# Bias copied into accumulators, and the weight loads of a two-MLP block reordered

## The chip, the cores and the metric

The kernel runs on one core of a Trainium2 chip. The metric is the device time of one execution in microseconds (us), the median of several runs. TensorE is written PE, VectorE DVE, ScalarE ACT, GpSimd POOL and SyncE SP.

## The reference

The input x has 32 sequences of 128 tokens with 512 features, so 4096 rows; cond gives one row of 512 per sequence, and mask marks some tokens of each sequence. All is float32.

```python
emb = silu(t) @ ada_w + ada_b
shift, scale, gate_msa = split(emb, 3)
norm = layernorm(x) * (1 + scale[:, None]) + shift[:, None]
norm = where(m, norm, 0)
fwd = gelu(norm @ ssm_w1 + ssm_b1) @ ssm_w2 + ssm_b2           # exact gelu
bwd = gelu(norm @ bwd_w1 + bwd_b1) @ bwd_w2 + bwd_b2           # the flips cancel
x = x + gate_msa[:, None] * where(m, fwd + bwd, 0)
ff_ada = silu(t) @ ffada_w + ffada_b
shift_mlp, scale_mlp, gate_mlp = split(ff_ada, 3)
ff_norm = layernorm(x) * (1 + scale_mlp[:, None]) + shift_mlp[:, None]
h = gelu_tanh(ff_norm @ ff_w1 + ff_b1)
out = x + gate_mlp[:, None] * (h @ ff_w2 + ff_b2)
```

ssm_w1, bwd_w1, ssm_w2 and bwd_w2 are 512 x 512; ff_w1 is 512 x 1024 and ff_w2 is 1024 x 512. The first two MLPs act on masked tokens only, the last one ("the second MLP" of the change) on all tokens.

## The kernel before

**Two parts.** The opening (to about 94 us) computes fwd + bwd for the masked tokens alone. They are numbered in slots; 512 slots in four tiles of 128 are handled in the straight program, and a loop at the end of the program would take further ones. The main part then runs the second MLP over four pairs of two groups of four sequences. Its two matrix products use a scheme of seven block products in place of eight (P1 to P7), applied twice in the first product, so sums and differences of blocks of weights and of tokens are made beforehand on VectorE.

**Order.** The schedule is written by hand: within each engine, instructions run in program order. Functions such as `hidden` and `project` take dictionaries that say behind which step another operation is placed. All loads of weights go through SP's queue in program order. [...]

**The opening, step by step.**

- Slots are counted, the first two tiles of rows are gathered from x (`xc`), and modulation rows `mod1` are computed on PE. `of_slots` multiplies a 0/1 matrix by modulation rows and so gives each slot its sequence's shift, scale or gate, in PSUM; `modulated_by_strips` applies them on VectorE. `xn_late` are the tiles 2 and 3 after that.
- `hidden` and `hidden_of_tile` (L207, L644) give the hidden layers, 8 blocks of 128 features: 4 of fwd, 4 of bwd. `w2` holds ssm_w2 in its first four blocks and bwd_w2 in its last four. `gates_of_slots` makes the gates `gs` of all four tiles.
- `project` (L224) sums the 8 blocks of a tile into one PSUM bank, 16 records for one tile. The pool ps_o has three banks, ps_h three, ps_t two.
- The bias of the projection is b2 + b2b, which is added to b2 on VectorE (L761). `with_gated_bias` (L348, L349) multiplies it by the gate and adds it to the tile's rows of x, for each of the four tiles. `finish_slots` (tiles 0 and 1: L354, L355 and statistics) and `finish_late` (tiles 2 and 3: L1342, L1343) multiply the projection by the gate, add the rows and store them.
- Tiles 0 and 1 are stored with their mean and root into `x1_wide`. POOL waits for both stores and then gathers them over the eight sequences of pair 0 in `take_first_half` (L813), of whose rows only the masked ones are replaced.
- `fw1` and `fw2` are ff_w1 and ff_w2. `Weights.combine` (L376) makes block differences of them, `weight_sums` (L703) makes further ones, and `store_weight_sums` writes these to DRAM (`t_rows`), from where the main part reads them as `tw`.
- ffada_w gives `mod2` (L301 with pm_f), which `transposed_modulation` transposes (`ptr_mod`, L793) into modT.
- The eight sequences of pair 0 are normalised (L838). Side 0 (four sequences) is transposed in 32 x 32 blocks on VectorE and its rows are reordered by 16 DMAs (`turned`, half on SP, half on ACT), then scaled on ACT (L878). Side 1 is transposed on PE (`turn(k)`, L884), each of the four transposing 128 features of all four sequences, and scaled on VectorE (L876). `TokenBlocks.one` (L925) makes block sums, and the first product starts (L1056).

**Where the loads stand before.** SP's queue holds, after the conditioning weights and the first layers: two pairs of sequences (`load_raw`), ssm_w2, bwd_w2, the two biases, fw1 in one load, two more pairs, ffada_w, its biases, then stores of tiles 0 and 1 and of weight sums 3. fw2 is loaded in eight parts, each behind one gather: a POOL memset of one element (L139) makes it wait for the gather's issue.

**What is placed where.** Side 1's turns and the row DMAs before stand so:

```python
after = {4 + b: [turn_rows(b)] for b in range(4)}
after[0] = [transposed_modulation]
after[1] = [lambda: weight_sums(2)]
...
po_s2 = project(0, h1, w2, "s2", {2: turn(0), 4: turn(1), 6: turn(2)})
finish_late(2, po_s2)
po = project(1, h1, w2, "s3", {0: turn(3)}, (ps_h, "h"))
```

Of the kernel before, what the change touches and what calls it, by code (L numbers as in the profile page):

```python
# [22 lines left out]
def kernel(  # L23
# [193 lines left out]
    def project(i, h, w, name, between=None, bank=(ps_o, "o")):  # L217

        pool, tag = bank
        po = pool.tile([P, 512], F32, tag=tag, name=f"po_{name}_{i}")  # L220
        for f in range(HC):
            if between and f in between:
                between[f]()
            nc.tensor.matmul(po, h[f][:, ts(i, P)], w[:, f, :], start=(f == 0), stop=(f == HC - 1))  # L224
        return po
# [77 lines left out]
    def of_slots(picked, tiles, mod, kinds, banks, name):  # L303

        n = kinds.stop - kinds.start
        t = [
            pool.tile([P, 512], F32, tag=tag, name=f"{name}_{j}")[:, : len(tiles) * n * P].rearrange(
                "p (a m c) -> p a m c", m=n, c=P
            )
            for j, (pool, tag) in enumerate(banks)  # L310
        ]
        for at, c in enumerate(tiles):
            for j in range(KC):
                nc.tensor.matmul(
                    t[j][:, at],
                    picked[ts(j, B), ts(c, P)],
                    mod[ts(j, B), kinds],
                    start=True,
                    stop=True,
                )  # L320
        return t
# [14 lines left out]
    def gates_of_slots(tiles):  # L336
# [5 lines left out]
        for j in range(KC):  # L342
            nc.scalar.copy(t[:, :, ts(j, P)], strips[j][:, :, 0])
        return [t[:, n] for n in range(len(tiles))]

    def with_gated_bias(at, gate):
        t = tp.tile([P, D], F32, tag="t", name=f"bg_s_{at}")
        nc.vector.tensor_tensor(t, b2, gate, ALU.mult)  # L348
        nc.vector.tensor_tensor(xc[at], xc[at], t, ALU.add)  # L349

    def finish_slots(at, h1, gate):
        t = tp.tile([P, 1, D + 2], F32, tag="t", name=f"t_s_{at}")
        row = t[:, 0, :D]
        nc.vector.tensor_tensor(row, project(at, h1, w2, f"s{at}"), gate, ALU.mult)  # L354
# [215 lines left out]
    load_raw(1)  # L570
    load_blocks(w2[:, :KC], ssm_w2)
    load_blocks(w2[:, KC:], bwd_w2)
# [50 lines left out]
    b2 = ssm.tile([P, D], F32, name="b2")  # L623
    b2b = tp.tile([P, D], F32, tag="t", name="b2b")
    fb2 = const.tile([P, D], F32, name="fb2")
    for t, vec in ((b2, ssm_b2), (b2b, bwd_b2)):
        broadcast_rows(t, vec, nc.sync)
    nc.sync.dma_start(fw1, ff_w1.rearrange("(k p) f -> p k f", p=P))
# [5 lines left out]
    load_conditioning_bias(modb_f, ffada_b, range(3), nc.sync)  # L634
    ph_s = {}
# [45 lines left out]
    def in_blocks(t):  # L681
        return t.rearrange("p g (h f) -> p (g h) f", f=2 * P)
# [52 lines left out]

# [7 lines left out]
    for n in range(2):  # L743
# [5 lines left out]
    xn_late = [  # L749
        modulated_by_strips(  # L750
            xc[2 + c], strips, c, spare[1][:, c], mv_t[:, c, 0:1], rstd_t[:, c : c + 1]
        )
        for c in range(2)
    ]
    h1 += hidden(xT_s, NH, w1, 0, AF.Gelu, "s0", ssm, range(KC, HC))
    gs = gates_of_slots(range(NC))
    fw1_of = Weights(fw1, KC // 2, FF // 2, t_1)
    fw1_of.combine(0, 1, 2, 3)
    for n in range(2, 4):
        own_statistics(raw[n], 2, f"x_{n}")  # L760
    nc.vector.tensor_tensor(b2, b2, b2b, ALU.add)  # L761
    b2_row = dram.tile([1, D], F32, name="b2_row")
    for c in range(2):
        with_gated_bias(c, gs[c])
    finish_slots(0, h1, gs[0])
    total, start_at, more_i, col_l = count_more()
    for c in range(2, NC):
        with_gated_bias(c, gs[c])
    finish_slots(1, h1, gs[1])
# [8 lines left out]
    modulation_matmuls(pm, ada_f, 0, 3, range(KC))  # L778
    modulation_rows(pm, mod2, modb_f, 0, 3)
    t = in_blocks(group_of_tiles("tw_3"))  # L780
    t_sum[3] = [t[:, :4], t[:, 4:]]
    weight_sums(3)
    store_weight_sums(3)
# [3 lines left out]
    weight_sums(1)  # L787
# [21 lines left out]
    def take_first_half(p, xs, which=range(2 * G), behind=None):  # L809
        slots = NH if p == 0 else NS  # L810
        for i in which:
# [9 lines left out]
            if behind:  # L821
                behind(i)
# [464 lines left out]
    def load_fw2_part(k):  # L1287
        load_behind_gathers(fw2[:, k : k + 1], ff_w2[ts(k, P)])

    take_first_half(0, x_of[0], range(2 * G), load_fw2_part)  # L1290
# [28 lines left out]
    def combine_behind_weight_sums():  # L1319
# [4 lines left out]
    after = {4 + b: [turn_rows(b)] for b in range(4)}  # L1324
    after[0] = [transposed_modulation]
    after[1] = [lambda: weight_sums(2)]
    after[4].insert(0, normalised_of_side_0)
    after[7] += [
        normalised_of_side_1,
        lambda: weight_sums(4),  # L1330
        combine_behind_weight_sums,
        lambda: store_weight_sums(4, 1, 2),
        lambda: x_of.update({1: [load_side(1, 0, spare), None]}),
    ]
# [5 lines left out]
    def finish_late(at, po):  # L1340
        t = tp.tile([P, D], F32, tag="t", name=f"t_s_{at}")
        nc.vector.tensor_tensor(t, po, gs[at], ALU.mult)  # L1342
        nc.vector.tensor_tensor(t, t, xc[at], ALU.add)  # L1343
        nc.sync.dma_start(x1_rows[ts(at, P), :], t)

    po_s2 = project(0, h1, w2, "s2", {2: turn(0), 4: turn(1), 6: turn(2)})
    finish_late(2, po_s2)
    po = project(1, h1, w2, "s3", {0: turn(3)}, (ps_h, "h"))
# [3 lines left out]
    finish_late(3, po)  # L1352
# [288 lines left out]
```

## Time and profile before

| what | value |
|---|---|
| median of 3 runs | 464.37 us (464.25 to 467.19) |
| the profiled execution's own time | 466.65 us |
| its span, first to last instruction | 464.9 us |
| mean granted TensorE clock | 0.992 |
| PE busy | 448.4 us (96%) |
| DVE busy | 334.7 us (72%) |
| ACT busy | 175.4 us (38%) |
| POOL busy | 163.5 us (35%) |
| moved by DMA | 70.96 MB, mean 153 GB/s |

The profile is of one execution, and its clock starts at the span's start. "Idle before, releaser" in its lines is the time that an engine stood still before an instruction and what ended it. The granted clock is 1.00 at full speed. A DMA's time to landing runs from its issue to its last completion.

### The profile page before, as it was taken

What the parts mean: (1) busy time and instruction counts of PE and PEld (TensorE: products, weight loads), DVE (VectorE), ACT (ScalarE), POOL (GpSimd) and SP (SyncE); (2) the same over time, 40 slices, a digit from 0 to 9 for tenths busy, and PEclk for the clock granted to TensorE, in tenths of its full rate; (3) what the DMA queues carried; (4) which work ended last, traced back from release to release, by engine and by line L of the source; (5) the groups of instructions that cost most, each with busy time, mean ns of one, the idle gap of its engine ahead of it and who ended that gap; (6) DMA issues with size and microseconds to landing.
All of it is one profiled execution on the core that took longest, in us unless ns stands there. A gap on an engine that the chain in (4) does not pass through costs nothing.

```text
span 464.9 us, 6219 instructions
## 1 busy us (share of the span) xinstructions
PE 448.4 (96%) x2160; PEld 371.7 (80%) x2160; DVE 334.7 (72%) x573; ACT 175.4 (38%) x384; POOL 163.5 (35%) x161
## 2 busy tenths in 40 slices
PE   8999878989999999999999999999999999999996
PEld 3785465468888888888888888888888888888884
DVE  4676986779869857996687489967873996433645
ACT  3121110465365273254543723535537144562000
POOL 4210146418964000289720004897100025660000
PEclk9999979999999999999999999999999999999999
DMA  7999269974405661934067529330764342222022
GB/s 232 383 394 401 80 177 210 273 273 150 158 9 187 99 123 43 338 115 163 3 206 103 100 70 340 100 145 2 222 98 89 125 169 80 79 77 106 0 82 103
DMA packets 83468, 70.96 MB, mean 153 GB/s; under 512 B 63224, under 2 KB 64584, under 8 KB 82410
## 3 DMA queue, kind: packets, MB, share of 16 engines
q1 hardware_dynamic: 68502, 58.61, 40.7%
q0 software_dynamic: 4160, 10.54, 6.6%
q10 hardware_dynamic: 10772, 1.39, 2.1%
q8 instruction: 18, 0.29, 0.2%
q14 instruction: 16, 0.13, 0.1%
HBM read 56.84 MB, written 13.70 MB: 152 GB/s over the span
## 4 chain that ended last, share of the span: by engine, by line
PE 78%; DMA 7%; DVE 7%; issue 2%; ACT 2%; SPq 1%; POOL 1%; POOLq 0%; DVEq 0%
PE a_o L1243 23%; PE a_m L1056 19%; PE e_o L1243 18%; PE e_m L1056 15%; DMA fw<-in_L_cond_ff_w_dram 3%; DMA ada_a<-in_L_cond_ada_w_dram 2%; ACT xT L878 1%; POOL x L813 1%; DMA x<-x_wide,slot_i 1%; DMA t_rows<-x 1%; PE ph_s L644 1%; DVE t L376 1%; PE last L1243 1%; DMA x_wide<-t_s 1%; DVE xc L349 1%
## 5 line engine op out<-in xcount | busy, mean ns | idle before, releaser
L1107 POOL TENSOR_TENSOR ha<-p_m,ha 128x512 f32<-128x512 f32 x20 | 25.8, 1288 | 166.6 <-ACT ha L1114 157.3
L1243 PE MATMUL e_o<-fw,ha 128*128 128x256 f32 x256 | 57.9, 379 | 0.0
L878 ACT ACTIVATE xT<-xT,modT 128x128 f32<-128x128 f32 x112 | 44.1, 480 | 34.8 <-DMA xT<-xn 31.4
L1243 PE MATMUL a_o<-t,hb 128*128 128x256 f32 x240 | 54.1, 379 | 0.0
L1243 PEld LDWEIGHTS e_o<-fw,ha 128*128 128x128 f32 x256 | 48.6, 190 | 6.6
L1243 PEld LDWEIGHTS a_o<-t,hb 128*128 128x128 f32 x240 | 45.6, 190 | 6.2
L1018 ACT ACTIVATE hb<-hb,biasT 128x256 f32<-128x256 f32 x64 | 29.0, 501 | 27.9 <-POOL hb L1140 19.3
L1070 ACT COPY p_m<-e_m 128x512 f32<-128x512 f32 x27 | 15.8, 585 | 46.8 <-PE e_m L1056 46.8
L813 POOL DMA_INDIRECT x<-x_rows,slot_i x24 | 27.6, 1148 | 6.3 <-issue 5.1
L1107 POOL TENSOR_TENSOR hb<-p_m,hb 128x512 f32<-128x512 f32 x20 | 29.4, 1469 | 0.3
L1243 PE MATMUL a_o<-fw,ha 128*128 128x256 f32 x128 | 28.9, 379 | 0.0
L1243 PE MATMUL a_o<-t,s 128*128 128x256 f32 x128 | 28.9, 379 | 0.0
L1243 PE MATMUL e_o<-fw,s 128*128 128x256 f32 x128 | 28.9, 379 | 0.0
L224 PE MATMUL po_s<-w,h_s 128*128 128x512 f32 x64 | 28.6, 594 | 0.0
L1114 ACT COPY ha<-e_m 128x512 f32<-128x512 f32 x32 | 18.5, 579 | 25.7 <-PE e_m L1056 25.2
L1243 PEld LDWEIGHTS e_o<-fw,s 128*128 128x128 f32 x128 | 24.3, 190 | 3.3
L1243 PEld LDWEIGHTS a_o<-t,s 128*128 128x128 f32 x128 | 24.3, 190 | 3.3
L1243 PEld LDWEIGHTS a_o<-fw,ha 128*128 128x128 f32 x128 | 24.3, 190 | 3.3
L1081 DVE TENSOR_TENSOR e_m<-a_m,ha 128x512 f32<-128x512 f32 x20 | 13.9, 696 | 16.7 <-POOL ha L1107 6.6
L1018 ACT ACTIVATE ha<-e_m,biasT 128x256 f32<-128x256 f32 x48 | 20.0, 468 | 15.6 <-PE e_m L1056 14.3
L1056 PE MATMUL e_m<-s,fw 128*128 128x256 f32 x92 | 23.8, 382 | 1.7 <-DVE e_m L1081 1.7
L1056 PE MATMUL a_m<-xT,tw 128*128 128x256 f32 x96 | 24.6, 379 | 0.0
(235 smaller groups left out, 902.2 us busy)
## 6 DMA issues: line engine op xcount, KB each, us to landing
tw<-t_rows SPq DMA_DIRECT2D x16, 896.0 KB, 5.3
x<-in_x_dram SPq DMA_DIRECT2D x16, 512.0 KB, 6.6
gate<-gate_rows POOLq DMA_DIRECT2D x8, 1024.0 KB, 5.1
out_dram<-x SPq DMA_DIRECT2D x15, 512.0 KB, 3.2
xT<-xn SPq DMA_DIRECT2D x92, 64.0 KB, 2.3
ada_f<-in_L_cond_ffada_w_dram SPq DMA_DIRECT2D x4, 768.0 KB, 14.8
ada_a<-in_L_cond_ada_w_dram SPq DMA_DIRECT2D x4, 512.0 KB, 5.5
w<-in_L_cond_ssm_w_dram SPq DMA_DIRECT2D x2, 1024.0 KB, 7.8
```

The source lines that it names most:

```text
L224: nc.tensor.matmul(po, h[f][:, ts(i, P)], w[:, f, :], start=(f == 0), stop=(f == HC - 1))
L349: nc.vector.tensor_tensor(xc[at], xc[at], t, ALU.add)
L376: engine.tensor_tensor(out, x, y, ALU.subtract)
L813: nc.gpsimd.indirect_dma_start(out=raw[i // 2][:, i % 2] if p == 0 else xs[i // G][i % G // 2][:, i % 2], out_offset=None, in_=x1_rows if ...
L878: nc.scalar.activation(out, src, AF.Identity, bias=shift, scale=scale)
L1018: nc.scalar.activation(dst[:, n], src[:, n], AF.Gelu_apprx_tanh, bias=biasT[:, f : f + 1])
L1056: nc.tensor.matmul(bank[:, ts(n, QT)], self.w_block(j, product)[:, ts(n, P)], self.x_block(j, product), start=(product in ("P1", "P5") and ...
L1070: nc.scalar.copy(p5, e)
L1081: nc.vector.tensor_tensor(e, a, p5, add)
L1107: nc.gpsimd.tensor_tensor(self.place(RESULT[j], c), self.p5[j], other, ALU.add)
L1114: nc.scalar.copy(self.place(RESULT[j], c), src)
L1243: nc.tensor.matmul(part, src[:, k, ts(i, P)], w[product][:, k, :], start=(last and k == 0), stop=True, skip_group_check=True,)
```

## The change

Seven edits, all in the opening.

1. The bias goes into the accumulators. `seeded_with_bias` copies b2 (already with b2b added) by ACT into a bank of ps_o, for tiles 0, 1 and 2, and `project` then accumulates onto it without a start flag. Tile 3, in a bank of ps_h, gets the bias by one VectorE addition in `finish_late`. `with_gated_bias` is gone. The first seed is copied between the gates' matmuls and the copies of the gates, the two others behind them.
2. `of_slots` starts only on the first tile of a bank.
3. b2 and b2b are loaded before ssm_w2, and added between the two tiles of xn_late.
4. fw1 is loaded before bwd_w2. Its combination, weight sums 3 and their store stand before `finish_slots(0)`, and the statistics of the later pairs behind it.
5. fw2 is loaded in two halves: one behind ffada_w and its biases, one behind the stores of tiles 0 and 1. The loads behind gathers and their memsets are gone.
6. Weight sums 1 stand before mod2's rows and are stored there; weight sums 2 are stored where they are made. `count_more` moves up.
7. The row DMAs of side 0 stand later (behind hidden blocks 5, 6, 7), side 1's turns each two blocks earlier (in front of blocks 0, 2, 4 and 6 of project 2).

```diff
@@ -214,14 +214,26 @@
                 g()
         return h
 
-    def project(i, h, w, name, between=None, bank=(ps_o, "o")):
+    def project(i, h, w, name, between=None, bank=(ps_o, "o"), seeded=None):
 
         pool, tag = bank
-        po = pool.tile([P, 512], F32, tag=tag, name=f"po_{name}_{i}")
+        po = seeded or pool.tile([P, 512], F32, tag=tag, name=f"po_{name}_{i}")
         for f in range(HC):
             if between and f in between:
                 between[f]()
-            nc.tensor.matmul(po, h[f][:, ts(i, P)], w[:, f, :], start=(f == 0), stop=(f == HC - 1))
+            nc.tensor.matmul(
+                po,
+                h[f][:, ts(i, P)],
+                w[:, f, :],
+                start=(f == 0 and seeded is None),
+                stop=(f == HC - 1),
+                skip_group_check=seeded is not None,
+            )
+        return po
+
+    def seeded_with_bias(at):
+        po = ps_o.tile([P, 512], F32, tag="o", name=f"po_s{at}")
+        nc.scalar.copy(po, b2)
         return po
 
     def gated(po, bias, gate, name):
@@ -315,8 +327,9 @@
                     t[j][:, at],
                     picked[ts(j, B), ts(c, P)],
                     mod[ts(j, B), kinds],
-                    start=True,
+                    start=(at == 0),
                     stop=True,
+                    skip_group_check=True,
                 )
         return t
 
@@ -339,19 +352,17 @@
             pick, tiles, mod1, slice(2, 3), 2 * [(ps_o, "o")] + 2 * [(ps_t, "tr")], f"gate_s{tiles[0]}"
         )
         t = ssm.tile([P, len(tiles), D], F32, tag="gs", name=f"gs_{tiles[0]}")
-        for j in range(KC):
-            nc.scalar.copy(t[:, :, ts(j, P)], strips[j][:, :, 0])
-        return [t[:, n] for n in range(len(tiles))]
-
-    def with_gated_bias(at, gate):
-        t = tp.tile([P, D], F32, tag="t", name=f"bg_s_{at}")
-        nc.vector.tensor_tensor(t, b2, gate, ALU.mult)
-        nc.vector.tensor_tensor(xc[at], xc[at], t, ALU.add)
-
-    def finish_slots(at, h1, gate):
+
+        def to_sbuf():
+            for j in range(KC):
+                nc.scalar.copy(t[:, :, ts(j, P)], strips[j][:, :, 0])
+
+        return [t[:, n] for n in range(len(tiles))], to_sbuf
+
+    def finish_slots(at, po, gate):
         t = tp.tile([P, 1, D + 2], F32, tag="t", name=f"t_s_{at}")
         row = t[:, 0, :D]
-        nc.vector.tensor_tensor(row, project(at, h1, w2, f"s{at}"), gate, ALU.mult)
+        nc.vector.tensor_tensor(row, po, gate, ALU.mult)
         nc.vector.tensor_tensor(row, row, xc[at], ALU.add)
         own_statistics(t, 1, f"s_{at}_x1")
         nc.sync.dma_start(x1_wide[ts(at, P), :], t[:, 0])
@@ -568,8 +579,11 @@
 
     load_raw(0)
     load_raw(1)
+    b2 = ssm.tile([P, D], F32, name="b2")
+    b2b = tp.tile([P, D], F32, tag="t", name="b2b")
+    for t, vec in ((b2, ssm_b2), (b2b, bwd_b2)):
+        broadcast_rows(t, vec, nc.sync)
     load_blocks(w2[:, :KC], ssm_w2)
-    load_blocks(w2[:, KC:], bwd_w2)
     pick_slots(1)
 
     slot_of = adap.tile([B, S], F32, name="slot_of")
@@ -620,18 +634,16 @@
     fw2 = fwp.tile([P, HC, D], F32, name="fw2")
     t_1 = fwp.tile([P, 3, KC // 2, FF // 2], F32, name="t_1")
     t_2 = fwp.tile([P, 3, HC // 2, D // 2], F32, name="t_2")
-    b2 = ssm.tile([P, D], F32, name="b2")
-    b2b = tp.tile([P, D], F32, tag="t", name="b2b")
     fb2 = const.tile([P, D], F32, name="fb2")
-    for t, vec in ((b2, ssm_b2), (b2b, bwd_b2)):
-        broadcast_rows(t, vec, nc.sync)
-    nc.sync.dma_start(fw1, ff_w1.rearrange("(k p) f -> p k f", p=P))
+    load_blocks(fw1, ff_w1)
+    load_blocks(w2[:, KC:], bwd_w2)
     load_raw(2)
     load_raw(3)
     ada_f = adap.tile([P, KC, 3 * D], F32, tag="ada", name="ada_f")
     modb_f = adap.tile([P, 3, P], F32, tag="modb", name="modb_f", bufs=1)
     load_ada(ada_f, ffada_w, range(KC), 3 * D)
     load_conditioning_bias(modb_f, ffada_b, range(3), nc.sync)
+    load_blocks(fw2[:, :KC], ff_w2[:D])
     ph_s = {}
 
     def hidden_of_tile(f, c):
@@ -732,7 +744,7 @@
         nc.vector.tensor_scalar(col_l, slot_col[:, 0:1], start_at, None, ALU.add)
         return total, start_at, more_i, col_l
 
-
+    total, start_at, more_i, col_l = count_more()
     h1 = []
     for f in range(KC):
         hidden_of_tile(f, 1)
@@ -746,27 +758,32 @@
     strips = of_slots(
         pick, (2, 3), mod1, slice(0, 2), 3 * [(ps_o, "o")] + [(ps_t, "tr")], "part_s2"
     )
-    xn_late = [
-        modulated_by_strips(
-            xc[2 + c], strips, c, spare[1][:, c], mv_t[:, c, 0:1], rstd_t[:, c : c + 1]
+    xn_late = []
+    for c in range(2):
+        xn_late.append(
+            modulated_by_strips(
+                xc[2 + c], strips, c, spare[1][:, c], mv_t[:, c, 0:1], rstd_t[:, c : c + 1]
+            )
         )
-        for c in range(2)
-    ]
+        if c == 0:
+            nc.vector.tensor_tensor(b2, b2, b2b, ALU.add)
     h1 += hidden(xT_s, NH, w1, 0, AF.Gelu, "s0", ssm, range(KC, HC))
-    gs = gates_of_slots(range(NC))
+    gs, gates_to_sbuf = gates_of_slots(range(NC))
+    po_s = [seeded_with_bias(0)]
+    gates_to_sbuf()
+    po_s += [seeded_with_bias(at) for at in (1, 2)]
     fw1_of = Weights(fw1, KC // 2, FF // 2, t_1)
     fw1_of.combine(0, 1, 2, 3)
+    t = in_blocks(group_of_tiles("tw_3"))
+    t_sum[3] = [t[:, :4], t[:, 4:]]
+    weight_sums(3)
+    store_weight_sums(3)
+    b2_row = dram.tile([1, D], F32, name="b2_row")
+    finish_slots(0, project(0, h1, w2, "s0", seeded=po_s[0]), gs[0])
     for n in range(2, 4):
         own_statistics(raw[n], 2, f"x_{n}")
-    nc.vector.tensor_tensor(b2, b2, b2b, ALU.add)
-    b2_row = dram.tile([1, D], F32, name="b2_row")
-    for c in range(2):
-        with_gated_bias(c, gs[c])
-    finish_slots(0, h1, gs[0])
-    total, start_at, more_i, col_l = count_more()
-    for c in range(2, NC):
-        with_gated_bias(c, gs[c])
-    finish_slots(1, h1, gs[1])
+    finish_slots(1, project(1, h1, w2, "s1", seeded=po_s[1]), gs[1])
+    load_blocks(fw2[:, KC:], ff_w2[D:])
     nc.sync.dma_start(b2_row, b2[0:1, :])
     broadcast_rows(fb2, ff_b2, nc.sync)
 
@@ -776,15 +793,12 @@
     mod2 = const.tile([P, 3, P], F32, name="mod2")
     pm = ps_h.tile([P, 512], F32, tag="h", name="pm_f")
     modulation_matmuls(pm, ada_f, 0, 3, range(KC))
+    weight_sums(1)
+    store_weight_sums(1)
     modulation_rows(pm, mod2, modb_f, 0, 3)
-    t = in_blocks(group_of_tiles("tw_3"))
-    t_sum[3] = [t[:, :4], t[:, 4:]]
-    weight_sums(3)
-    store_weight_sums(3)
     early.close()
     xtp = straight.enter_context(tc.tile_pool(name="xtp", bufs=1, side="right"))
     sp = straight.enter_context(tc.tile_pool(name="sp", bufs=1, side="right"))
-    weight_sums(1)
     modT = const.tile([P, KC, 2 * B], F32, name="modT")
 
     def transposed_modulation():
@@ -806,7 +820,7 @@
     fw2_of = Weights(fw2, HC // 2, D // 2, t_2)
 
 
-    def take_first_half(p, xs, which=range(2 * G), behind=None):
+    def take_first_half(p, xs, which=range(2 * G)):
         slots = NH if p == 0 else NS
         for i in which:
             b = 2 * p * G + i
@@ -818,8 +832,6 @@
                 bounds_check=slots - 1,
                 oob_is_err=False,
             )
-            if behind:
-                behind(i)
 
     def gate_tile(p, side):
         t = gp.tile([P, G, D], F32, tag=f"g{side}", name=f"gate_{p}_{side}", bufs=1)
@@ -1284,10 +1296,7 @@
                 self.store(c, 1)
 
 
-    def load_fw2_part(k):
-        load_behind_gathers(fw2[:, k : k + 1], ff_w2[ts(k, P)])
-
-    take_first_half(0, x_of[0], range(2 * G), load_fw2_part)
+    take_first_half(0, x_of[0])
     xT = [new_xT(0, side) for side in range(2)]
     gate_rows = dram.tile([B, D], F32, name="gate_rows")
     for j in range(KC):
@@ -1321,35 +1330,40 @@
         nc.gpsimd.tensor_copy(done, t_sum[4][1][0:1, 2, 0:1])
         fw2_of.combine(0, 1, engine=nc.gpsimd)
 
-    after = {4 + b: [turn_rows(b)] for b in range(4)}
-    after[0] = [transposed_modulation]
-    after[1] = [lambda: weight_sums(2)]
-    after[4].insert(0, normalised_of_side_0)
-    after[7] += [
-        normalised_of_side_1,
-        lambda: weight_sums(4),
-        combine_behind_weight_sums,
-        lambda: store_weight_sums(4, 1, 2),
-        lambda: x_of.update({1: [load_side(1, 0, spare), None]}),
-    ]
+    after = {
+        0: [transposed_modulation, lambda: weight_sums(2), lambda: store_weight_sums(2)],
+        3: [normalised_of_side_0],
+        5: [turn_rows(0)],
+        6: [normalised_of_side_1, turn_rows(1)],
+        7: [
+            turn_rows(2),
+            turn_rows(3),
+            lambda: weight_sums(4),
+            combine_behind_weight_sums,
+            lambda: store_weight_sums(4),
+            lambda: x_of.update({1: [load_side(1, 0, spare), None]}),
+        ],
+    }
     h1 = hidden(xT_t, NH, w1, 0, AF.Gelu, "s1", ssm, after=after)
     nc.scalar.activation(warm, biasT[0:1, 0:1], AF.Gelu_apprx_tanh)
     for k in range(KC):
         scaled(0, xT[0], k)
 
-    def finish_late(at, po):
+    def finish_late(at, po, bias=None):
         t = tp.tile([P, D], F32, tag="t", name=f"t_s_{at}")
+        if bias is not None:
+            nc.vector.tensor_tensor(t, po, bias, ALU.add)
+            po = t
         nc.vector.tensor_tensor(t, po, gs[at], ALU.mult)
         nc.vector.tensor_tensor(t, t, xc[at], ALU.add)
         nc.sync.dma_start(x1_rows[ts(at, P), :], t)
 
-    po_s2 = project(0, h1, w2, "s2", {2: turn(0), 4: turn(1), 6: turn(2)})
-    finish_late(2, po_s2)
-    po = project(1, h1, w2, "s3", {0: turn(3)}, (ps_h, "h"))
+    finish_late(2, project(0, h1, w2, "s2", {2 * k: turn(k) for k in range(KC)}, seeded=po_s[2]))
+    po = project(1, h1, w2, "s3", bank=(ps_h, "h"))
     of_x[0] = TokenBlocks(0, xT)
     for j in (1, 2, 3, 4):
         of_x[0].one(j)
-    finish_late(3, po)
+    finish_late(3, po, b2)
     first_half.close()
     hp = straight.enter_context(tc.tile_pool(name="hp", bufs=1))
     gp = straight.enter_context(tc.tile_pool(name="gp", bufs=1))
```

## The prediction

> **What bounds the kernel now.** First the table of stages (busy time of each engine per stretch) and the page's busy row: from 110 us on TensorE has no gap worth naming until the tail, so a change in the opening is worth what it moves the start of that stretch, one for one, and no more than TensorE loses before it.
>
> ```profile
> PE 448.4 (96%) x2160; PEld 371.7 (80%) x2160; DVE 334.7 (72%) x573; ACT 175.4 (38%) x384; POOL 163.5 (35%) x161
> ...
> 50.00:60.00 10.00, 6.11 (x50) 3.31 (x48) 9.45 (x24) 1.67 (x5) 0.55 (x1) 0.93 0.15 56
> 60.00:70.00 10.00, 9.04 (x33) 7.69 (x34) 8.48 (x15) 1.42 (x3) 5.28 (x8) 0.73 0.72 213
> ...
> 110.00:120.00 10.00, 10.00 (x48) 8.75 (x48) 9.77 (x20) 5.21 (x10) 8.76 (x8) 1.00 0.16 32
> ```
>
> Columns: stretch, length, then busy time (count) of PE, PEld, DVE, ACT, POOL, then PE clock, DMA share, GB/s. From 50 to 70 VectorE is full, TensorE is not, its clock falls. The DMA view of 30 to 62 us (40 slices of 0.8 us) shows a pause of transfers there, with the full rate of about 410 until 46 us and a thin rest until 52.4:
>
> ```profile
> GB/s 410 415 410 410 410 410 410 392 392 392 412 399 422 433 384 438 407 415 422 407 207 131 106 93 52 20 19 5 0 0 0 98 382 177 0 0 0 0 0 139
> ```
>
> Next TensorE's waits up to 112 us (in total, times, longest):
>
> ```profile
> PE ptr_mod L793 <- DVE mod L301: 4.8, 1, 4.8
> PE ptr L884 <- DVE xn L838: 2.3, 2, 1.3
> PE e_m L1056 <- DVE e_m L1081: 1.7, 2, 1.1
> PE e_m L1056 <- ACT e_m L1102: 0.5, 1, 0.5
> ```
>
> Who makes VectorE late is in the chain (start, length, what) and in the timeline:
>
> ```profile
> 24.92 14.40 DMA fw<-in_L_cond_ff_w_dram
> ...
> 60.88 2.98 DMA x_wide<-t_s
> ...
> 75.14 4.42 DMA x<-x_wide,slot_i
> ...
> 60.35 0.56 DVE L301 TENSOR_TENSOR mod<-pm_f,modb_f 128x384 f32<-128x384 f32 x1
> 60.96 0.69 PE L793 MATMUL ptr_mod<-ident,mod 128*128 128x128 f32 x2 [4.85 <-DVE mod L301]
> 61.44 14.19 PE L207 MATMUL ph_s<-xT_s,w 128*128 128x256 f32 x56
> ...
> 80.19 0.33 PE L884 MATMUL ptr<-ident,xn 128*128 128x128 f32 x1 [1.34 <-DVE xn L838]
> 93.69 1.03 PE L1056 MATMUL a_m_alone<-xT,fw 128*128 128x256 f32 x4
> ```
>
> So the order is: fw1 lands at 39.3; VectorE combines it, adds gated biases and finishes two tiles until 60.1; only then is mod ready (TensorE idle 4.85) and the second tile stored; the store lands at 63.87, eight gathers follow to 79.56, and project 2 goes on behind turn(0) at 80.35. The first product begins at 93.69 and loses 2.9 us more up to its group at 107.79: that group starts 14.1 after 93.69, where 13 groups of 0.863 are 11.2.
>
> **What the Trainium skill says.** "TensorE: Matmul & The Clock Gate", Part 1: the clock halves after an idle activity window of about 3.4 us, and windows run freely. The trace agrees: with one idle stretch of 4.85 us the clock was 0.50 over 58.54:65.37, in which TensorE worked 4.41 us, so 2.2 us were lost. "DMA: Bandwidth & Descriptors", "Queues, rings and completion order": each DMA engine takes one queue's descriptors in ring order and alternates between queues by packets. No row shows that per engine; it fits the fw1 load, which was issued at 24.92 and landed 14.4 later with the queue full. "PSUM — Partial Sum Buffer", "The four PSUM rules": a matmul without the first-flag accumulates onto what another engine wrote where the bank's bits are set, which is why of_slots now keeps its start flag for the first tile; this costs no instruction. The copy's price comes from the trace:
>
> ```profile
> L1182 ACT COPY a_o<-fb x8: 575/585/592, 133.5 to 416.5; 128x512 f32<-128x512 f32 x8
> L224 PE MATMUL po_s<-w,h_s 128*128 128x512 f32 x64 | 28.6, 594 | 0.0
> ```
>
> **The change part by part.** Times below are on the profile's clock.
>
> 1. Loads. fw1 goes ahead of bwd_w2 (1024 KB). The DMA view shows 410 GB/s here, so it lands 2.6 earlier, about 36.8. bwd_w2 lands where fw1 did, 39.3; project 0 wants it at its fifth block, at 40.8 (below), so 1.5 us cover it. b2 and b2b only pass ssm_w2, which has over 6 us to spare. SP runs well ahead of the data (fw1 issued at 24.92), so the moved issues cost nothing.
>
> 2. Bias. Eight L348/L349 operations leave VectorE (about 0.65 each in sequence: 5.3 us). One addition (0.69) comes on the late tile path and b2 + b2b goes between the two tiles of xn_late (0.62). Three ScalarE copies of 0.58 come in; ScalarE waits 12.50 us before its L199 copy at 51.07, which hides them. The moved addition is not free: the gates of L314 reuse the banks that the second tile reads, so the gates end at 37.3 for 36.67, and both projections (16 records of 0.433 each, 6.9 us) end at 44.2 and 51.1, not 50.44. Seed 0 waits for the same tile (35.8), is done at 36.4 and is not late.
>
> 3. VectorE, 36.8 on. Combine 5.0 to 41.8, weight sums 3 (1.28 + 0.95, less overlap: 2.1) to 43.9. finish_slots(0) now waits for TensorE at 44.2 and takes 2.5, to 46.8; statistics of two raw pairs 3.6, to 50.4; finish_slots(1) from 51.2 to 53.7. That end was 60.1. count_more's seven operations (1.1 us) lie in the 2.39 us wait for x at 22.97, for nothing. Then 0.3 + 2.1 (weight sums 1, now ahead of mod) + 0.6: mod at 56.7.
>
> 4. TensorE, 51.1 on. Transposes 1.0, modulation 2.7, hidden f=0 2.0: 56.8. ptr_mod no longer waits. That gives back 4.85 and the 2.2 of the half clock. Seven more hidden blocks at 1.73 (ScalarE's steps at 67.10, 68.83 and 70.55): done at 69.4, for 75.6.
>
> 5. Stores and gathers. Half of fw2 goes into the pause, but the pause has to hold more. Behind the thin rest, which keeps a few engines busy until 52.4, stand in SP's queue fw2's first half (2.6), the weight sums 3 (896 KB, 2.2), and x_wide, x_rows of tile 0 (1.3). On the engine that ends last this is 58.5; x_wide of tile 1, issued at 54.3 after POOL's root (0.55), lands there at about 59.2, against 57.3 on an empty queue (2.98 after its issue, as before). An estimate, and the first uncertain term: between 57.3 and 60.5 (one more transfer of 1.3 in front). The first gather starts 0.75 later, as at 64.63 before: 60.0. The gathers step at 1.30 (69.93, 71.23, 72.53 ...); the memsets between them vanish but lie inside the step. The last is issued at 69.3 (0.2 for a slow one), lands 4.2 later (median 3.7, longest 4.4): 73.5. Normalising 0.55 and the last transpose 0.3 make turn(0) ready at 74.4, for 80.35.
>
> 6. The new wait. turn(0) now stands ahead of project 2, where before two blocks of it (1.73) ran first. TensorE is free at 69.4 and waits until 74.4, except for three short transposes: about 5 us, the length that cost 2.2 us of clock before. Depending on where the free-running window lies the loss is 1.0 to 2.7; I take 1.9. Behind it: 32 records of 0.433 (13.85) and three turns of 0.43 (1.3). The first product starts at 74.4 + 15.15 + 1.9 = 91.5, for 93.69: 2.2 gained.
>
> 7. What else could be late then. The other side's rows: VectorE ends side 0 at about 69.4, the 16 DMAs of turned took from 75.1 to 90.1 before, in a queue with fw2 and six weight-sum stores. The stores of weight sums 1 and 2 now go out by about 66, so I put the rows at 82, and ScalarE's 16 operations (6.3) end at 88.5: in time. ScalarE's gelu of f=6 and f=7 stand behind row issues, but project wants them only from about 81. Of the 2.9 us lost in the first product, the seed on ScalarE (0.8 with the restart) and the wait at 100.86 (1.3) were owed to this backlog and go, but for 0.2; the one at 107.79 (0.8) is VectorE's own sequence from L1086 on and stays. Gain 1.9. SP's load of the second fw2 half is behind x_rows, lands by about 63, and is wanted by POOL's combine only after 76.
>
> Sum: 2.2 + 1.9 = 4.1. The profiled execution took 466.65 with a span of 464.9; its result would be 462.5. Against the median of the runs shown, 464.37, this is 460.3. About 1% (4.6 us) is what can be told from no change here, so the forecast lies just inside.
>
> **Rivals.** *No cold clock, lighter queue.* If x_wide lands 3 us after its issue, everything from the gathers on is 1.9 earlier, the wait is 3 us, and the clock may hold (another 1.9): 464.37 - 4.1 - 3.8 = 456.5; with one of the two, about 458.4. For it: the pause measured 5 to 19 GB/s in its last slices. Against: four transfers ahead.
>
> *Gain stays a wait.* The first product's losses remain although all starts earlier, or the clock takes the full 2.7: 464.37 - 2.2 + 0.8 to 464.37 - 2.2, so about 462.5. For it: VectorE still has all L925, L985 and L989 work there.
>
> *Slower: gathers starved.* Gathers 1 and 2 before were 1.69 and 2.31 apart, while stores and fw2 filled the queue at over 380 GB/s. Now fw2's second half and two pairs of weight-sum stores (2.8 MB) leave in just the gathers' time. With 2.3 us for each of seven gaps, turn(0) is 7.0 later, and TensorE, with nothing ahead of it, waits all of that: 464.37 - 4.1 + 7.0 = 467.3. It decides above 1.30 + 4.1/7 = 1.9 us a gap. Against: the long gaps ended at 68.63 although fw2 went on loading.
>
> That the change does not do what it says is no rival here: the written order puts the seeds, fw1 and the halves of fw2 where it claims.
>
> **How the numbers follow.** Forecast 0.42 (459 to 462), lighter queue 0.30, gain stays a wait 0.18, starved gathers 0.10. Range 456.6 to 464.4: it cuts the better half of the second case and the slower one. Faster by over 1% (below 459.7): most of the second case and a third of the first, 0.42; slower by over 1% (above 469.0): the far end of the last, 0.04; the rest 0.54.
>
> **What would show it.** In the changed profile: the fw1 combine at 36.8; no wait at ptr_mod and clock 1.0 through 60:69; x_wide of tile 1 landing at 59; gathers 1.3 apart; one wait of turn(0) of 4 to 5 us near 70 and a half clock behind it; the first product at 91.5. If that wait is under 3 us or the clock holds, I am too slow by 2 to 4; if gathers are over 1.9 apart, too fast.

## The result and the profile after

The changed kernel takes 462.66 us (median; 460.93 to 464.05), the kernel before 464.78 beside it; the ratio is 0.9946, 95% interval 0.9929 to 0.9962. That is 2.1 us by the medians and 2.5 by the ratio: a small gain that is clear of the noise, inside the range forecast, with a time 2.4 us above the forecast of 460.3. The profiled execution took 461.21 with a span of 459.5, so it is 1.45 quicker than its own median, while that of before, 466.65, was about 2 slower than its median. The two pages therefore differ by more than the two kernels do.

The three longest waits of TensorE up to 112 us of the changed kernel (in total, times, longest):

```profile
PE ptr L896 <- DVE xn L850: 4.0, 1, 4.0
PE pm_keep_clock L446 <- DVE zeros L441: 1.3, 1, 1.3
PE e_m L1068 <- DVE e_m L1093: 0.6, 1, 0.6
```

The 4.8 us at ptr_mod are gone; one wait of 4.0 at turn(0) has come. The chain of waits through that stretch (start, length, what):

```profile
54.12 4.94 DMA x_wide<-t_s
...
59.92 6.30 DMA x<-x_wide,slot_i
...
66.87 0.55 DVE xn L850
...
71.65 1.43 DVE xn L850 x3
...
73.12 0.93 PE ptr L896 x2
74.05 3.00 PE po_s L224 x4
```

The store of tile 1 takes 4.94 (2.98 before), the first gather takes 6.30 to land. VectorE, idle until 66.87, then normalises both sides without a pause, and it is this sequence that lets turn(0) go, not the last gather. Behind it four records of project 2 take 3.00 instead of 1.73. The table by stretches says why (stretch, length, PE, PEld, DVE, ACT, POOL, PE clock, DMA share, GB/s):

```profile
60.00:70.00 10.00, 8.20 (x38) 6.86 (x37) 3.03 (x6) 1.50 (x4) 7.87 (x8) 1.00 0.73 276
70.00:80.00 10.00, 7.54 (x22) 3.80 (x23) 8.52 (x19) 2.21 (x3) 6.52 (x8) 0.83 0.66 99
...
73.08:76.50 3.42, 3.38 (x6) 1.56 (x7) 3.42 (x8) 0.95 (x2) 0.84 (x2) 0.50 0.88 128
```

The first product, in the timeline (start, busy time, what, and in brackets the idle time before it):

```profile
90.22 1.03 PE L1068 MATMUL a_m_alone<-xT,fw 128*128 128x256 f32 x4
...
102.49 1.13 PE L1068 MATMUL e_m<-s,fw 128*128 128x256 f32 x4 [0.62 <-DVE e_m L1093]
```

It starts at 90.22 for 93.69, and the group that stood at 107.79 stands at 102.49.

### The profile page after: what moved, and what is told of

The parts are those of the page before. It is cut to its first block, busy times and chain, and to the rows that moved or that the text cites. A ratio compares the mean times of both kernels' runs of the same rounds, so it can differ in the third digit from the quotient of the medians.

```text
span 459.5 us, 6188 instructions
## 1 busy us (share of the span) xinstructions
PE 447.8 (97%) x2160; PEld 371.0 (81%) x2160; DVE 330.3 (72%) x566; ACT 177.4 (39%) x387; POOL 161.3 (35%) x153
## 4 chain that ended last, share of the span: by engine, by line
PE 87%; DMA 5%; DVE 5%; issue 1%; SPq 1%; POOL 1%; DVEq 0%; POOLq 0%
PE a_o L1255 23%; PE a_m L1068 20%; PE e_o L1255 18%; PE e_m L1068 15%; PE po_s L224 6%; DMA x<-in_x_dram 3%; DMA x<-x_wide,slot_i 1%; DMA x_wide<-t_s 1%; PE last L1255 1%; DVE xn L850 1%; PE a_m_alone L1068 1%; PE pm_keep_clock L446 1%; PE ptr L896 0%; DVE xn L1313 0%; DVE x L340 0%
## 5 line engine op out<-in xcount | busy, mean ns | idle before, releaser
L224 PE MATMUL po_s<-w,h_s 128*128 128x512 f32 x64 | 29.7, 617 | 0.0
```

## The experiments

My first theory was that the gain was eaten at the new wait of turn(0) and by the half clock behind it. The rivals were that the profile of before was itself a slow one; that full queues around the gathers cost the rest; and that one of the two parts of the change carries the gain alone. Each ratio is to the kernel before on the same chip, with its 95% interval.

**The kernel before again** (e0, no edit).

> The kernel before, unchanged, to see how its own runs spread. My theory: the wait of 4.85 us at ptr_mod and the half clock behind it (6.83 us in its profile, mean clock 0.992) are part of nearly every run, so the clocks lie at 0.991 to 0.993, the times within 464 to 467, ratio 1.000 within 0.3%. Rival (the profile of before was simply a slow one): the clocks of its runs fall into two groups, some at 0.995 or more, and those runs are about 1.7 us or more faster than the others; the median run then had less to win than the profiled one.

Measured: 464.71 us, ratio 1.000 (0.9982 to 1.0018). The clocks form no two groups with their own times: over the 34 runs of this kernel, those at 0.996 took 464.2 to 465.1, those at 0.990 took 464.6 to 467.0. That speaks against the rival in the form expected. But its profiled execution took 464.99, 1.66 less than the one that the prediction read. The wait at ptr_mod is the same 4.8 with the clock at half over 6.82 us behind it; the first product differs:

```profile
93.66 1.03 PE L1056 MATMUL a_m_alone<-xT,fw 128*128 128x256 f32 x4
...
104.15 1.10 PE L1056 MATMUL e_m<-sx,tw 128*128 128x256 f32 x4 [0.56 <-DMA tw<-t_rows]
...
105.95 1.11 PE L1056 MATMUL e_m<-s,fw 128*128 128x256 f32 x4
```

The start is the same (93.66 for 93.69), but the last group shown, the one that stood at 107.79, comes 12.3 later and not 14.1: 1.1 us lost there and not 2.9. So 1.8 of the 2.9 came in one of the two executions and not in the other. The 16 operations on the other side's rows on ScalarE, which stand ahead of the waits in question, start at 90.14 in the first profile and at 88.09 in this one. Of the 34 runs, 8 took 465.9 us or more, as that first execution did (466.65); whether they have the same stall is not shown.

**The bias part alone** (e4: the kernel before with the seeds, the early loads of b2 and b2b, and nothing of the new order).

```diff
+        nc.scalar.copy(po, b2)                      # seeded_with_bias, three tiles
...
-    for c in range(2):
-        with_gated_bias(c, gs[c])
-    finish_slots(0, h1, gs[0])
+    finish_slots(0, project(0, h1, w2, "s0", seeded=po_s[0]), gs[0])
```

> The kernel before with the bias part of the change alone: b2 and b2b loaded early, seeds in three accumulators, bias of the last tile added at its end; the loads of fw1 and fw2 and the weight sums stay as before. By my sum VectorE loses 5.3 us of work ahead of mod and gains none: tile 1 finished near 55 for 60.1, mod near 57, ptr_mod waits under 1 us, the clock holds there; x_wide of tile 1 has an empty queue ahead of it and lands 3 us after its issue; gathers from 58.5, turn(0) ready near 73 with two blocks in front of it. If the bias carries the gain, the median is at or below that of the whole change: 459.5 to 462.5. Rival (the order of the loads carries it, because VectorE cannot start before fw1 is there at 39.3): mod no earlier than 59, ptr_mod waits 3 us or more, median 464 or above.

Measured: 459.73 us, ratio 0.9888 (0.9859 to 0.9917): 5.0 us faster than before by the medians, and faster than the whole change. Its waits of TensorE up to 112 and its chain:

```profile
PE ptr L896 <- DVE xn L850: 3.0, 2, 2.2
...
PE ptr L896 <- issue: 0.6, 1, 0.6
```
```profile
53.85 3.22 DMA x_wide<-t_s
...
68.49 4.63 DMA x<-x_wide,slot_i
73.14 0.56 DVE xn L850
73.74 0.47 PE ptr L896
```

No wait at ptr_mod is left, although fw1's combine begins only at 38.44. x_wide lands 2.0 earlier than in the whole change (57.07 for 59.06), and its first gather, issued at 57.85, is normalised at 62.03, 4.2 us after its issue, where the whole change has 6.95. The order of the loads was not needed for the gain. Nor is the quicker first gather what makes the bias part faster in this pair of profiles: as the last lines show, VectorE now waits for the last gather, which lands 4.63 us after its issue, and project 2 goes on at 74.01, level with the whole change (74.05). But two of its blocks (1.73 us) ran before turn(0), and the first product begins at 88.72, 1.5 earlier.

**The order alone** (e5: the changed kernel, its loads, weight sums and turns, with the gated bias on VectorE again).

```diff
-    finish_slots(0, project(0, h1, w2, "s0", seeded=po_s[0]), gs[0])
+    nc.vector.tensor_tensor(b2, b2, b2b, ALU.add)
+    for c in range(2):
+        with_gated_bias(c, gs[c])
+    finish_slots(0, project(0, h1, w2, "s0"), gs[0])
```

> The changed kernel without the bias part: the gated bias is worked out by VectorE for all four tiles as in the kernel before, the loads, weight sums and turns stay as changed. My sum with VectorE free at 36.0: combine 5.0, weight sums 2.1, bias 3.3, tile 0 2.5, statistics 3.6, bias 2.6, tile 1 2.5: tile 1 finished at 57.6 for 60.1, mod at 60.6, so ptr_mod waits 4.8 us as before; x_wide lands near 62, turn(0) ready near 77, hidden done at 75.6, a wait of 1.5. First product 92 for 93.69: 463 to 464.5, ratio 0.996 to 1.000. If the order of the loads carries a gain of its own it is 462 or less; if it costs on its own what it costs beside the bias part (2.9 us), 466 to 468.

Measured: 464.98 us, ratio 0.9999 (0.9983 to 1.0016): nothing. Its waits name the old place and the new one together:

```profile
PE ptr_mod L813 <- DVE mod L313: 4.8, 1, 4.8
...
PE ptr L902 <- DVE xn L856: 0.9, 1, 0.9
```

VectorE gets as late at mod as before. The next runs ask which part of the order takes back what the seeds give.

**Turns later** (e1: the changed kernel with two blocks of project 2 ahead of turn(0) again).

```diff
-    finish_late(2, project(0, h1, w2, "s2", {2 * k: turn(k) for k in range(KC)}, seeded=po_s[2]))
-    po = project(1, h1, w2, "s3", bank=(ps_h, "h"))
+    finish_late(2, project(0, h1, w2, "s2", {2 * k + 2: turn(k) for k in range(KC - 1)}, seeded=po_s[2]))
+    po = project(1, h1, w2, "s3", {0: turn(KC - 1)}, bank=(ps_h, "h"))
```

> The changed kernel, with the turns of side 1 back where they were (at blocks 2, 4, 6 of project 2 and ahead of project 3), so that two blocks (1.73 us) run before turn(0) waits. My theory: what the change had to give it lost at this wait (4.0 us in its profile) and in the half clock behind it (1.7 us in the profile, more in other runs). The wait shrinks to about 2.3 us, the clock holds in most runs (0.997 or more), the first product begins at 86.8 to 88.5 for 90.22, and the median is 459.3 to 461.0, ratio to before 0.988 to 0.992. Rival (the rest of the way is set by the rows of the other side, not by TensorE): the time gained comes back as a wait inside project 2 or at the first product, median about 462.5, ratio 0.995.

Measured: 461.21 us, ratio 0.9907 (0.9880 to 0.9933), 1.45 better than the change by the medians, 1.8 by the ratios, whose intervals just overlap. The wait shrank from 4.0 to 2.7. The clock did not hold in its profile (6.83 us of half clock, shown in the last section), so the first product began at 89.85, and not by 88.5 as expected.

**Work inside the wait** (e2: the changed kernel with four matmuls of no use between hidden and project 2).

```diff
+    pm_busy = ps_h.tile([P, 512], F32, tag="h", name="pm_busy")
+    for k in range(KC):
+        nc.tensor.matmul(pm_busy, ident, w2[:, k, :], start=True, stop=True)
```

> The changed kernel, with four matmuls of 128x512 whose result is not used put between the last hidden block and project 2: 3.5 us of work on TensorE inside the wait of 4.0 us for turn(0). Nothing else moves, so this measures the clock alone. My theory (half clock behind the wait in every run, one window or two): clock 0.998 or more in all runs, first product at about 88.5 for 90.22, median 1.7 to 2.5 us below the changed kernel, 460 to 461. Rival (the clock is not what makes the runs differ): median 462.5, spread as before; and if the four reach past the end of the wait, up to 0.5 slower.

Measured: 462.16 us, ratio 0.9930 (0.9902 to 0.9959). The clock was 0.997 to 1.000 in all its runs and yet they spread over 459.66 to 463.73. The gain expected from the clock did not come: 0.5 us by the medians, and the intervals overlap. Its profile shows one way in which it is lost. The first product begins at 89.02, 1.2 before the changed kernel's, and VectorE takes this back much later, between the groups at 366.38 and 370.87:

```profile
370.87 1.13 PE L1068 MATMUL e_m<-xT,fw 128*128 128x256 f32 x4 [0.53 <-DVE e_m L1112]
```

Here the two kernels are level again, and the spans end within 0.1 us of each other. In this kernel the clock explains neither the size of the result nor the spread.

**turn(0) first, on the bias part** (e9: the bias part alone with the turns as the change has them; the lines of e1 the other way round).

> The bias part alone, with turn(0) ahead of project 2 and the others at blocks 2, 4, 6, as the change has them. If the place of turn(0) costs what undoing it gave on the changed kernel (1.45 us), the median is 461.0 to 461.6; with the wait of 2.2 longer by the two blocks (1.73 us) and a half clock of two windows for one up to 462.7. If the place is worth nothing, 459.7.

Measured: 461.78 us, ratio 0.9920 (0.9894 to 0.9947). This agrees with e1 from the other side: 2.1 us by the medians, 1.5 by the ratios, though by the ratios alone the two intervals overlap.

**fw2's first half in the pause, on the bias part** (e10).

```diff
     load_conditioning_bias(modb_f, ffada_b, range(3), nc.sync)
+    load_blocks(fw2[:, :KC], ff_w2[:D])
...
-    take_first_half(0, x_of[0], range(2 * G), load_fw2_part)
+    take_first_half(0, x_of[0], range(2 * G), lambda k: k < KC or load_fw2_part(k))
```

> The bias part alone, with the first half of fw2 (1024 KB) loaded in the pause ahead of the stores of x_wide, and only the second half in parts behind gathers 5 to 8. If the load in the pause holds up x_wide: it lands up to 1.3 us later than 57.07, gathers and turn(0) with it, median 460.5 to 461.2. If the pause is free, or the lighter queue behind the gathers brings back as much: 459.2 to 460.0.

Measured: 460.95 us, ratio 0.9901 (0.9872 to 0.9931). The first gather goes out at 58.43 for 57.85. The sign and the size are as expected, but the intervals overlap, so this run alone doesn't decide.

**Both halves of fw2 behind the gathers** (e3b: the changed kernel).

```diff
-    load_blocks(fw2[:, :KC], ff_w2[:D])
...
-    load_blocks(fw2[:, KC:], ff_w2[D:])
...
     take_first_half(0, x_of[0])
+    load_behind_gathers(fw2, ff_w2)
```

> The changed kernel with both halves of fw2 loaded behind the last gather of x_wide instead of in the pause. The bias part alone reached 459.73, so the order of the loads takes back about 2.9 us. Theory Q (the queue: fw2's halves and the weight sums stand in front of x_wide and of the first gathers): x_wide of tile 1 lands at about 57.3 for 59.06, the first gather within 4 us for 6.3, turn(0) is ready 1.2 to 1.8 us before 73.1, and the median comes to 460 to 461.5. Theory T (the place of turn(0) ahead of project 2 is what costs; the queue only decides which of two waits is seen): gathers earlier, but the median within 0.5 of 462.66. If POOL's combine of fw2 becomes late instead, a wait for tw or fw shows between 100 and 130 us and the median is above 462.7.

Measured: 465.03 us, ratio 1.0000 (0.9986 to 1.0013), slower than the change. The mechanism of theory Q is there: the first gather is normalised 3.7 us after its issue (58.48 to 62.21), and the first product begins at 88.21, 2.0 earlier. Then it stops. Its chain and its waits show the place:

```profile
57.20 12.12 issue
69.33 0.38 SPq L136
...
70.42 11.52 DMA t_rows<-t
...
81.96 0.59 SPq L905
```
```profile
PE e_m L1066 <- ACT e_m L1112: 2.3, 1, 2.3
PE ptr L894 <- DVE xn L848: 1.9, 3, 1.3
PE a_m_alone L1066 <- ACT xT L888: 1.5, 1, 1.5
```

SP stands 12 us on the load that waits for the last gather, and with it everything written behind that load. The stores of weight sums follow 2 MB of fw2 and take 11.52, the other side's rows are issued behind them, and ScalarE's 16 operations on these rows start at 87.28 for 82.27. The first product waits for them.

**Turns later and fw2 behind** (e6: the edits of e1 and e3b together).

> The changed kernel with two blocks ahead of turn(0) again and both halves of fw2 behind the gathers: both suspected costs taken out together, what is left of the change is the bias, fw1 ahead and the weight sums 3 and 1 early. If the two account for the 2.9 us between the whole change and its bias part, the median is that of the bias part, 459.2 to 460.3. If it stays at 461 or more, the early weight sums and their stores (896 KB each into the same pause) carry the rest.

Measured: 465.38 us, ratio 1.0009 (0.9997 to 1.0021). The same blockage as in e3b, larger because TensorE gets there earlier (a_m_alone waits 3.4 for ScalarE). Its question was spoiled by the load's place, so it was asked again with fw2 in eight parts, as before.

**Turns later and fw2 in eight parts** (e8: the changed kernel; left of the order are fw1 ahead of bwd_w2, the early weight sums with their stores, and the smaller moves of edits 4, 6 and 7, such as the later row DMAs).

```diff
-    load_blocks(fw2[:, :KC], ff_w2[:D])
...
-    load_blocks(fw2[:, KC:], ff_w2[D:])
...
-    take_first_half(0, x_of[0])
+    take_first_half(0, x_of[0], range(2 * G), load_fw2_part)
```

> The changed kernel with the turns where they were (blocks 2, 4, 6 and project 3) and fw2 again in eight parts behind the gathers: what is left beside the bias part is fw1 ahead of bwd_w2 and the weight sums 3, 1 and 2 with their stores early. If the place of the turns and of fw2 make up the whole difference of 2.9 us between the change and its bias part, the median is 459.3 to 460.3. If the early weight sums and their stores cost by themselves, it stays where the turns alone brought it, 461.2, or above.

Measured: 459.71 us, ratio 0.9867 (0.9840 to 0.9893), against 0.9946 (0.9929 to 0.9962) for the change: 3.7 us by the ratios, with intervals apart, and 2.95 by the medians. It beats both kernels, and is level with the bias part alone. The first gather is quick again; in the timeline:

```profile
56.83 1.70 POOL L825 DMA_INDIRECT x<-x_wide,slot_i  x1 [3.81 <-DMA x_wide<-t_s]
...
61.10 0.55 DVE L850 TENSOR_SCALAR xn<-x 128x512 f32<-128x512 f32 x1 [3.54 <-DMA x<-x_wide,slot_i]
```

It is normalised 4.3 us after its issue, project 2 goes on behind turn(0) at 72.31 (74.05 in the change), and the first product begins at 87.33. So the turns and fw2 together account for what the order took back; fw1, the early weight sums and the smaller moves cost nothing that can be seen.

**Four blocks ahead of turn(0)** (e7 is the bias part, e11 is e8, each with these two lines in place of its own).

```diff
+    finish_late(2, project(0, h1, w2, "s2", {4: turn(0), 6: turn(1)}, seeded=po_s[2]))
+    po = project(1, h1, w2, "s3", {0: turn(2), 2: turn(3)}, (ps_h, "h"))
```

> The bias part alone, with four blocks of project 2 ahead of turn(0) instead of two, and turns 2 and 3 inside project 3: a try for a better version. If TensorE's wait at turn(0) still sets the end (2.2 us, and a half clock of 1.7 behind it), the first product begins 1.7 to 3.4 us earlier and the median is 456.5 to 458. Rival: the 16 ScalarE operations on the other side's rows (82.52 to 88.8 in the profile of the bias part) are the next bound, the first product begins no earlier than 88 and the median stays at 459 to 460.

> As the run with fw2 in parts behind the gathers, but with four blocks of project 2 ahead of turn(0): a try for a version below 459.7. With weight sums stored early the wait for tw of 1.5 us that the bias part showed with four blocks should go, so 458 to 459.3; if the other side's rows set the first product, 460 or above.

Measured: 460.15 us, ratio 0.9879 (0.9857 to 0.9901), and 459.66, ratio 0.9867 (0.9843 to 0.9891): no better than two blocks. In e11 the wait at turn(0) is down to 1.0 and the first product begins at 84.63, 5.6 before the changed kernel's; its waits up to 112, and ScalarE's and TensorE's timeline:

```profile
PE e_m L1068 <- ACT e_m L1114: 1.9, 1, 1.9
PE e_m L1068 <- DVE e_m L1093: 1.0, 2, 0.6
PE ptr L896 <- DVE xn L850: 1.0, 1, 1.0
```
```profile
82.48 6.27 ACT L890 ACTIVATE xT<-xT,modT 128x128 f32<-128x128 f32 x16 [2.95 <-DMA xT<-xn]
88.65 0.57 ACT L1114 COPY e_m<-a_m_alone 128x512 f32<-128x512 f32 x1
```
```profile
89.27 1.13 PE L1068 MATMUL e_m<-xT,fw 128*128 128x256 f32 x4 [1.89 <-ACT e_m L1114]
```

The copy into e_m, with which the first product starts one of its sums (not one of the bias seeds), stands behind the 16 operations on the other side's rows on ScalarE. These end near 88.7, hardly other than in the changed kernel (88.54), though TensorE is 5.6 us ahead. Of the 5.6 us only 0.8 are left in the span (458.7 for 459.5). In this profile ScalarE's rows are the next bound of the opening.

## Why the prediction was right, and where it was wrong

- *The number.* It was right by its range. 456.6 to 464.4 held everything from a gain of 7.8 us to none, and the gain measured, 2.1 to 2.5, is little over half of the 4.1 forecast. The nearest of its cases was the one given 0.18, "gain stays a wait" (462.5).
- *Part 1.* fw1's combine began at 36.0, put at 36.8. Right, and of no use: the bias part alone does without it. Its combine begins at 38.44, and yet tile 1 is taken up at 50.58, in the changed kernel at 50.39, when project 1 ends.
- *Parts 2 and 3.* The gates ended at 36.4, put at 37.3; the projections at 50.4, put at 51.1; tile 1 was finished at 53.0, put at 53.7; mod at 55.6, put at 56.7. Right in kind; each came 0.7 to 1.1 earlier than put, beginning with the gates (0.9).
- *Part 4.* ptr_mod has no wait left and the clock is 1.00 over 60 to 70, as put. This is what the seeds buy: the wait is gone in e4 and back in e5. Hidden ended at 68.2, put at 69.4; the sum as written, 56.8 and seven blocks of 1.73, gives 68.9.
- *Part 5.* The times held: x_wide landed at 59.06 (59.2 put), the first gather went out at 59.92 (60.0), steps of 1.30, the last at 69.15 (69.3), the last normalisation ended at 73.5 (74.05), and project 2 went on at 74.05 (74.4). The reason did not: I let the last gather end the wait. In this profile it was the first gather, 6.30 us in landing, which held VectorE's seven remaining normalisations back; they then ran end to end. In e4, where the first gather is quick, the last gather does end the wait (VectorE stands 1.96 us for it), at the same time.
- *Part 6.* The wait was 4.0 (about 5 put), the half clock lost 1.7 (1.9 put), the first product began at 90.22 (91.5 put). So 3.5 us were gained in this execution where 2.2 were put. But this execution was 1.45 quicker than the median; with that taken off, about 2 remain, which is the number put. No profile shows a median run, so this agreement may be luck. The clocks point to a longer half clock in most runs: another 3.41 us of it lowers the mean clock over 460 us by 0.0037, and of the 18 runs the 5 at 0.994 or above (the profiled one has 0.996) have a median of 461.26, the 13 below it 462.80. e2, with the clock at 0.997 or more in every run and a median of 462.16, says that the clock is not all of it.
- *Part 7, the step that failed.* "Of the 2.9 us lost in the first product" 1.9 were booked as a gain. The loss after is 1.05 (102.49 - 90.22 less 11.2), as put. The loss before, in the other profile of it, is 1.1. The mechanism named, ScalarE late with the other side's rows, is what the two profiles differ in (90.14 and 88.09); that it stands in every run is what failed. A stall of one execution was taken for a property of the kernel and then, with the rest of the sum, taken off the median of runs of which most are quicker than that execution. Without this term the sum is 2.2, and 464.37 - 2.2 is 462.2, beside 462.66 measured.
- *The rivals.* "Gain stays a wait" had the number, 462.5: the first product's loss stayed what it is in the second profile of before (1.05 for 1.1). "Lighter queue" was not what the change does, but what e8 makes of it. "Starved gathers" did not come at the steps between gathers, where I looked, but at the first landing, and cost less than the 7.0 us put.
- *The clock.* "TensorE: Matmul & The Clock Gate" in the Trainium skill, Part 1, puts the half clock behind an idle window of about 3.4 us. The trace agrees in the length of one half-clock stretch (3.42) and not in the condition: already in the profile of before the half clock begins at 58.54, 2.4 us into the idle stretch, and the last section shows shorter waits. That a clock regained would be worth its full loss at the end, on which the "lighter queue" case leaned, e2 did not bear out (0.5 us by the medians for 1.7 to 2.5 expected).
- The premise that the start of the first product counts one for one up to the end holds for the changed kernel against e9 or the bias part (differences of 0.4 and 1.5 kept to the end). It fails once TensorE passes ScalarE's rows near 88.7 (e11 keeps 0.8 of 5.6; e7 and e8, which begin at 87.65 and 87.33, keep 1.0 of 2.6 and 1.8 of 2.9), and once in a later stretch (e2).

What stays open: how the 3.7 us (2.95 by the medians) split between the turns and fw2 (1.5 to 2.1 and 0.6 to 1.9 by the pairs of runs), what makes the changed kernel's median 1.45 slower than its profiled execution, and whether fw2's second half alone holds up the first gather in the changed kernel or only together with all the weight-sum stores. One pair of these stores by itself does not: in e8 it goes out at 54.71 and 55.15 (896 KB), ahead of the first gather, and that gather is quick.

## What to carry to other kernels

Look at a second profile of the kernel before booking one of its stalls as a gain, and keep profile and median apart: terms that one execution alone shows come off that execution alone. Run the parts of a change one by one, because here one part gave 5 us, the other nothing by itself, and together they gave half. A wait that moves ahead of the work that used to cover it costs about that work's length (1.5 to 2.1 us here for two blocks of 1.73 together), and a load that waits holds all that is written behind it on its queue (12 us in e3b).

## What the runs showed of the hardware

- A wait shorter than 3.41 us, the shortest half-clock stretch of the opening, is enough for the half clock. In e1 a wait of 2.7 us led to two such stretches, in e11 one of 1.9 to one (columns as in the table by stretches, e1 first):

```profile
72.07:78.90 6.83, 6.38 (x13) 3.25 (x14) 5.34 (x12) 0.95 (x2) 3.83 (x5) 0.50 0.75 115
```
```profile
90.58:94.00 3.42, 3.01 (x9) 1.85 (x7) 3.22 (x6) 1.52 (x3) 0.00 (x0) 0.50 0.32 96
```

What goes before them is little work, not none. Cut between 15 and 110 us into pieces of 3.41 us that fit its half-clock stretches, the 14 profiles show the clock fall to half 14 times. In the piece just before, TensorE had been busy for at most 1.52 us in 13 of them (0.66 in the changed kernel, 1.14 in e1, 1.52 in e11) and for 2.13 in one (e5). No piece behind which the clock stayed full shows less than 1.93. How many stretches follow is not settled by this: in e1 TensorE was busy for 2.96 us of the first one and a second followed, in e9 for 2.80 and none did.

- The landing of the first gather stands in two groups: 5.8 to 6.9 us (6.30 in the change, 5.77 in e1, 6.41 in e2, 6.94 in e5), and at most 3.4 to 4.6 from its issue to its use in e3b, e4 and e6 to e11. The first four have fw2's second half in one load, and the weight-sum stores, close behind x_wide; none of the others has that load there.
